# First layer of a two-layer model: a chunk's key-value sum ahead of its outputs, and the state updated by one VectorE operation per head

## The chip, the cores and the metric

The kernel runs on one core of a Trainium2 chip. The metric is the device time of one execution in microseconds; of the kernel before there are five runs, and their median counts. A profile is one more execution, recorded instruction by instruction. Engines are named as in the profile: PE (TensorE, matmuls; PEld are its weight loads), DVE (VectorE), ACT (ScalarE), POOL (GpSimd), SP (SyncE, which issues DMAs).

## The reference, cut to what matters

Two layers run one after the other on x of 2 x 2048 x 256. The change is in the attention of the first layer, a gated linear attention with two heads of 128:

```python
def step(S, inp):
    qt, kt, vt, gt = inp
    S = jnp.exp(gt)[..., None] * S + kt[..., None] * vt[..., None, :]
    ot = jnp.einsum('bhd,bhde->bhe', qt, S)
    return (S, ot)
```

The state S (128 x 128 per head) decays by a factor per row and takes in the outer product of key and value; the output is the query times the state. Beside it the first layer quantises the normed input in blocks of 32 (`_mx_quantize`) and multiplies it by a quantised weight. The output of the attention is gated, normed (`_layernorm`) and projected, and both are added to x. The second layer (softmax attention, then experts) follows and is not touched.

## The kernel before, in words

**Tiling.** The 4096 tokens are cut into 8 strips of 512 (`Strip`, 0 to 3 for the first sequence, 4 to 7 for the second), a strip into four chunks of 128. Inside a chunk the decay is folded into queries and keys, so that a chunk's output is two products per head: masked weights x values (`attn`, `v`), and query x state. The state is kept scaled so that one factor per row and head, `to_next`, carries it to the next chunk: new state = (state + keys x values) x `to_next`. The factor is a product of two columns of `spans`, which ScalarE fills in `queries()` (L675) before the strip's chunks run.

**A chunk (`chunk(n)`, L765 to L804).** One PSUM tile `both` (named o_ds_ps in the profile, two buffers) holds the outputs `o_ps` and the key-value sums `ds_ps`. TensorE does, per head, weights x values and query x state into `o_ps`, then both heads' keys x values into `ds_ps`. Each float32 product is two matmul instructions in the trace, some 0.11 us apart. VectorE makes `to_next` (L792, 128x2) and adds state and `ds_ps` for both heads into `sum` (L796, 128x256). ScalarE scales `sum` by `to_next`, one operation per head (L799, 128x128), which is the new state. VectorE then multiplies the gate by `o_ps` into `og` (L801) and takes its statistics (L119, L121). Chunk 0 of a sequence has no state before it (`none`), and the last chunk of a sequence makes none.

**What sets the order.** The strips are woven together by hand in the loop from L867. For strip s the order of pieces is: `weights()` of s; `values_gates()` of s+1 (products vf_ps); then chunk 0, chunk 1, `queries()` of s+1 (products q_ps and c_ps, on VectorE `arg` L680 and L681 and q L683, on ScalarE `ls` and the exponential of `arg` L682), chunk 2, chunk 3; between them the four steps of the quantisation of s+1 (`mx_steps`, L149), which alternate VectorE (L180 to L188, L193, L196) and GpSimd (L191, L194, L197); then the norm of `og` (`norm_o`: GpSimd L128, VectorE L130), the query and key products of the second layer for s-1 (qk_ps), the transposes of `og` (tr, L565), `keys()` of s+1, `sum_up()` (y_ps), and so on. The matmuls are kept in program order by `mm` (L514). On VectorE, ScalarE and GpSimd a scheduler puts the instructions in an order of its own when the kernel is built, except for those pinned; each engine then runs its list in order. Waits are counts of finished instructions on another engine.

**Strips that differ.** Strip 0 also quantises the weight (`quantised_weight`, tile wd, and its copies by ScalarE L596). Strip 4 starts a sequence. Strip 7 has no strip after it, so its four chunks follow each other with no quantisation and no queries between them.

Of the kernel before, what the change touches and what calls it, by code (L numbers as in the profile page):

```python
# [53 lines left out]
F32 = mybir.dt.float32  # L54
# [3 lines left out]
ALU = mybir.AluOpType  # L58
# [3 lines left out]
P = 128  # L62
# [5 lines left out]
HG = 2  # L68
# [184 lines left out]
@with_exitstack  # L253
def usual_way(ctx, tc, a, out, c, blocks):
    nc = tc.nc
    keep = ctx.enter_context(tc.tile_pool(name="keep", bufs=1))
    acc = keep.tile([P, NT, E], F32, tag="acc", name="acc")
    la = keep.tile([P, NT, NE], F32, tag="la", name="la")
    norms = keep.tile([P, 1, NSTRIP], F32, tag="norms", name="norms")
    spans = keep.tile([P, NSTRIP, HG, 4, 2], F32, tag="spans", name="spans")  # L260
    operands = Operands(nc, keep, a, c)
    ready = Constants(nc, keep, a, c)

    fill = Fill(nc, keep, a, out, c)

    def besides(s):

        if s == 0:
            fill.begin()
            operands.make_first()  # L270
            ready.load()
        elif s < NSTRIP - 2:
            fill.rows(s - 1, NSTRIP - 3)
        elif s == NSTRIP - 2:
            operands.load_first()

    with tc.tile_pool(name="proj", bufs=1) as pool:
        layer0(tc, a, acc, spans, c, operands, Projections(tc, pool, a, c, norms, la), besides)
    later = ctx.enter_context(tc.tile_pool(name="later", bufs=1))
    routing = Routing(nc, later, a, c)  # L280
    attention(tc, a, out, acc, la, norms, spans, c, operands, ready, routing, blocks)
# [217 lines left out]
def layer0(ctx, tc, a, acc, spans, c, operands, projections, besides):  # L499
# [6 lines left out]
    nc = tc.nc  # L506
# [3 lines left out]
    p2 = ctx.enter_context(tc.tile_pool(name="l0p2", bufs=2))  # L510
# [3 lines left out]
    def mm(*args, **kwargs):  # L514
        tc.keep_in_program_order(nc.tensor.matmul(*args, **kwargs))  # L515
# [82 lines left out]
    class Strip:  # L598


        def __init__(self, s):
            self.s = s
            self.ts = slice(4 * s, 4 * s + 4)
            self.x = acc[:, self.ts, :]
            self.first = s % (NSTRIP // B) == 0
            self.last = (s + 1) % (NSTRIP // B) == 0

        def norm_x(self):
            self.xn = p2.tile([P, 4, E], F32, tag="xn", name="xn", bufs=1)
            norm = LayerNorm(nc, p2, expo, "x")  # L610
            norm.see(self.x, 0)
            norm.apply(self.xn, self.x)
            nc.gpsimd.tensor_tensor(
                self.x, self.x, ffnb.unsqueeze(1).to_broadcast([P, 4, E]), ALU.add
            )
# [121 lines left out]
        def weights(self):  # L737
# [24 lines left out]
            self.og = p2.tile([P, 4, E], F32, tag="og", name="og", bufs=1)  # L762
            self.norm = LayerNorm(nc, p2, expo, "o")

        def chunk(self, n):  # L765

            nonlocal state
            s = self.s
            both = ps_s.tile([P, 2, HG, P], F32, tag="sm", name="o_ds_ps")
            o_ps, ds_ps = both[:, 0, :, :], both[:, 1, :, :]  # L770
            none = self.first and n == 0
            for h in range(HG):
                hs = slice(h * P, (h + 1) * P)
                mm(
                    o_ps[:, h, :], lhsT=self.attn[:, h * 4 + n, :], rhs=self.v[:, n, hs],
                    start=True, stop=none,
                )
                if not none:
                    mm(
                        o_ps[:, h, :], lhsT=self.q[:, h, n * P : (n + 1) * P],  # L780
                        rhs=state[:, h, :], start=False, stop=True,
                    )
            if not (self.last and n == 3):
                for h in range(HG):
                    hs = slice(h * P, (h + 1) * P)
                    mm(
                        ds_ps[:, h, :], lhsT=self.kt[:, n, hs], rhs=self.v[:, n, hs],
                        start=True, stop=True,
                    )
                after = spans[:, s, :, n + 1, 0] if n < 3 else spans[:, s + 1, :, 0, 0]  # L790
                to_next = p2.tile([P, HG], F32, tag="to_next", name="to_next")
                nc.vector.tensor_tensor(to_next, spans[:, s, :, n, 1], after, ALU.mult)  # L792
                sum_ = ds_ps
                if not none:
                    sum_ = p2.tile([P, HG, P], F32, tag="sum", name="sum")
                    nc.vector.tensor_tensor(sum_, state, ds_ps, ALU.add)  # L796
                new = p2.tile([P, HG, P], F32, tag="state", name="state", bufs=3)
                for h in range(HG):
                    nc.scalar.mul(new[:, h, :], sum_[:, h, :], to_next[:, h : h + 1])  # L799
                state = new  # L800
            nc.vector.tensor_tensor(  # L801
                self.og[:, n, :], self.gate[:, n, :], o_ps.rearrange("p h d -> p (h d)"), ALU.mult
            )
            self.norm.see(self.og[:, n : n + 1, :], n)  # L804
# [43 lines left out]
        def greatest(self):  # L848
            projections.greatest(self.s, self.squares, ps_m, mm)

    state = None
    nc.scalar.preload_act_table_set("natural_log_exp_and_others")
    strips = [Strip(s) for s in range(NSTRIP)]

# [12 lines left out]
    for s, now in enumerate(strips):  # L867
        after = strips[s + 1] if s + 1 < NSTRIP else None
# [1483 lines left out]
```

## Time and profile before

| what | us |
|---|---|
| median of 5 runs | 1775.18 (1772.32 to 1777.95) |
| the profiled execution, its time | 1772.8 |
| its span, first to last instruction | 1770.9 |
| first layer in it | up to about 450 |
| busy in the span: PE / DVE / ACT / POOL | 1671.4 / 694.3 / 804.7 / 392.3 |
| one strip (vf_ps of one to vf_ps of the next) | 50.1 |
| chunk 0 of strip 2 / of strip 7 begins | 163.2 / 406.8 |

A row of a timeline or of a chain begins with its start and its length in us from the start of the span; then come engine, line, operation, tile written <- tiles read, and shape. In square brackets stands how long the engine was idle before it and what ended that. A row of a tile or line view has min/median/max of one instruction in ns. A row of the waits has the total, the number of times and the longest, in us. A wait is put down to the event that came last before it ended, and this is only where the reader starts: that event can itself have been held up by an older one in its engine's queue, which the chain of waits follows back.

### The profile page before, as it was taken

Reading aid. Unit: us, or ns where it says so; the run is one execution under the profiler, and the core shown is the slowest. Engines: PE = TensorE matmul, PEld = TensorE weight load, DVE = VectorE, ACT = ScalarE, POOL = GpSimd, SP = SyncE. Lnnn points to the kernel's source line nnn. Section 1 sums busy time; section 2 is a strip of 40 time slices with the busy share of each in tenths; the row PEclk is TensorE's granted clock in tenths of the full one; section 3 lists DMA queues with packets and bytes.
Section 4 is the critical chain, followed back from the end, with each engine's and each line's share of the span. In section 5 each row is a group of like instructions: output and inputs, shape, how many; then the busy total and the mean of one; then the engine's idle time right before and its main releaser. Section 6 shows DMA issues by size and latency. Waiting matters only on the chain.

```text
span 1770.9 us, 31816 instructions
## 1 busy us (share of the span) xinstructions
PE 1671.4 (94%) x13314; PEld 1296.1 (73%) x13314; DVE 694.3 (39%) x1798; ACT 804.7 (45%) x1590; POOL 392.3 (22%) x350
## 2 busy tenths in 40 slices
PE   4699999998999989999999999999999999999995
PEld 2467666665666656766766688898888888889885
DVE  7877667653554663232242222222222222222221
ACT  2344554544778767978988911111111112111110
POOL 4332222211200003324300012222222222222211
PEclk9899999999999999999999999999999999999998
DMA  9501114104600401442130175556555555557521
GB/s 268 154 24 38 50 50 101 50 24 110 137 10 1 78 13 63 101 111 66 51 124 14 43 269 169 164 176 214 176 178 188 181 182 194 164 177 237 164 84 17
DMA packets 82505, 204.33 MB, mean 115 GB/s; under 512 B 8624, under 2 KB 64304, under 8 KB 71728
## 3 DMA queue, kind: packets, MB, share of 16 engines
q0 software_dynamic: 24944, 138.33, 24.1%
q1 hardware_dynamic: 56304, 62.71, 13.2%
q8 instruction: 106, 1.74, 0.4%
q10 hardware_dynamic: 1104, 1.18, 0.2%
q14 instruction: 47, 0.39, 0.1%
HBM read 152.26 MB, written 49.92 MB: 114 GB/s over the span
## 4 chain that ended last, share of the span: by engine, by line
PE 83%; DVE 9%; ACT 4%; POOL 1%; DMA 1%; issue 1%; SPq 0%; POOLq 0%; DVEq 0%
PE h_ps L2113 27%; PE y_ps L2129 13%; PE sc L1687 11%; PE o_ps L1718 10%; PE y_ps L515 3%; PE qk_ps L515 3%; ACT pt L1693 3%; PE vf_ps L515 2%; PE f_ps L1670 2%; PE vg_ps L515 2%; PE tr L565 2%; DVE pt L1705 2%; PE g_ps L515 1%; PE o_tr L1644 1%; PE o_ds_ps L515 1%; PE x_ps L2091 1%
## 5 line engine op out<-in xcount | busy, mean ns | idle before, releaser
L1693 ACT ACTIVATE pt<-sc,shift 128x512 f32<-128x512 f32 (+3 forms) x832 | 464.7, 680 | 100.0 <-PE sc L1687 98.0
L2113 PE MATMUL h_ps<-va,qk 128*128 128x256 f32 (+1 forms) x2368 | 484.3, 365 | 0.0
L2113 PEld LDWEIGHTS h_ps<-va,qk 128*128 128x128 f32 x2368 | 425.4, 190 | 53.3 <-ACT va L2095 0.2
L2118 ACT ACTIVATE sg<-h_ps 128x256 f32<-128x256 f32 (+1 forms) x296 | 109.4, 370 | 593.5 <-PE h_ps L2113 591.7
L1687 PE MATMUL sc<-qk 32*128 32x256 f32 (+6 forms) x3680 | 277.9, 370 | 4.2 <-DVE onT L1664 1.7
L2119 DVE TENSOR_TENSOR larger<-sg,h_ps 128x256 f32<-128x256 f32 (+1 forms) x296 | 119.3, 403 | 355.4 <-ACT sg L2118 332.7
L1687 PEld LDWEIGHTS sc<-qk 32*128 32x128 f32 x3680 | 202.1, 187 | 63.4 <-ACT pt L1693 27.8
L1718 PE MATMUL o_ps<-pt,va 128*32 128x256 f32 (+7 forms) x3680 | 230.0, 353 | 17.5 <-DVE o_sb L1751 17.5
L1718 PEld LDWEIGHTS o_ps<-pt,va 128*32 128x32 f32 x3680 | 122.4, 110 | 97.0 <-issue 29.9
L2138 POOL DMA_INDIRECT out<-va,to x69 | 110.1, 1596 | 216.7 <-DMA out<-va,to 69.6
L1705 DVE TENSOR_TENSOR pt<-pt,keepmask 128x1024 f32<-128x1024 f32 x64 | 78.5, 1226 | 185.6 <-ACT pt L1693 185.6
L2129 PE MATMUL y_ps<-qk,larger 128*128 128x256 f32 x560 | 124.3, 379 | 1.0 <-DVE va L2134 1.0
L2129 PE MATMUL y_ps<-larger 128*128 128x256 f32 x544 | 120.4, 379 | 0.0
L2129 PEld LDWEIGHTS y_ps<-qk,larger 128*128 128x128 f32 x560 | 104.8, 190 | 14.8 <-DVE va L2134 1.4
L2134 DVE SCALAR_TENSOR_TENSOR va<-y_ps,wt,half_bias 128x256 f32<-128x256 f32 x69 | 30.4, 480 | 209.9 <-PE y_ps L2129 209.9
L2129 PEld LDWEIGHTS y_ps<-larger 128*128 128x128 f32 x544 | 102.0, 190 | 13.1
L2023 POOL DMA_INDIRECT table<-rows,place x64 | 65.8, 1028 | 172.8 <-DMA table<-rows,place 134.8
L2053 POOL DMA_INDIRECT qk<-in_wgateup,wrow x37 | 37.3, 1007 | 298.5 <-PE h_ps L2113 152.4
L515 PE MATMUL vf_ps<-qk,xnT 128*128 128x512 f32 x128 | 58.3, 609 | 0.0
L515 PE MATMUL o_ds_ps<-state,q 128*128 128x128 f32 x120 | 25.6, 296 | 22.8 <-ACT state L799 22.8
L515 PEld LDWEIGHTS vf_ps<-qk,xnT 128*128 128x128 f32 x128 | 24.1, 194 | 29.0 <-issue 27.0
L1675 DVE TENSOR_TENSOR acc<-acc,f_ps 128x512 f32<-128x512 f32 x32 | 22.0, 687 | 56.8 <-PE f_ps L1670 56.8
(246 smaller groups left out, 1715.0 us busy)
## 6 DMA issues: line engine op xcount, KB each, us to landing
xb<-table SPq DMA_DIRECT2D x32, 265.0 KB
qk<-qk SPq DMA_DIRECT2D x32, 256.0 KB
qk<-qk SPq DMA_DIRECT2D x64, 128.0 KB
table<-spare SPq DMA_DIRECT2D x3, 2120.0 KB
va<-v SPq DMA_DIRECT2D x4, 1208.0 KB
v<-v SPq DMA_DIRECT2D x8, 574.0 KB
normed<-xn SPq DMA_DIRECT2D x8, 512.0 KB
rows<-normed POOLq DMA_DIRECT2D x16, 256.0 KB
```

The costliest lines, as they stand in the source:

```text
L515: tc.keep_in_program_order(nc.tensor.matmul(*args, **kwargs))
L1687: nc.tensor.matmul(scs[r][:, at : at + q1 - q0], lhsT=heads[rows, 1, kb * P : (kb + 1) * P], rhs=heads[rows, 0, qt * QT + q0 : qt * QT + q ...
L1693: nc.scalar.activation(pt[:, r, 0:width], scs[r][:, 0:width], AF.Exp, bias=shift)
L1705: ins = nc.vector.tensor_tensor(part, part, mask[:, 1 - way, :].unsqueeze(1).unsqueeze(1).to_broadcast([P, 4, 2, P]), ALU.min,)
L1718: nc.tensor.matmul(o_ps[r * HR : (r + 1) * HR, to + q0 : to + q1], lhsT=va[:, kb, h * VC : h * VC + HR], rhs=pt[:, r, at : at + q1 - q0], ...
L2023: self.nc.gpsimd.indirect_dma_start(out=self.c.table, in_=rows[:, n, :], in_offset=None, out_offset=bass.IndirectOffsetOnAxis(ap=to[:, 2 * ...
L2053: e.nc.gpsimd.indirect_dma_start(out=w, out_offset=None, in_=e.a[name], in_offset=bass.IndirectOffsetOnAxis(ap=e.c.wrow[:, self.b : self.b ...
L2113: nc.tensor.matmul(ps[:, j, rows], lhsT=self.wgu[:, j, c, f * P : (f + 1) * P], rhs=self.xT[:, c, rows], start=c == 0, stop=c == 1,)
L2118: nc.scalar.activation(sg, ps[:, 0, rows], AF.Silu)
L2119: nc.vector.tensor_tensor(self.hT[:, f, rows], sg, ps[:, 1, rows], ALU.mult)
L2129: nc.tensor.matmul(ps[:, c, :], lhsT=self.hT[:, fc, c * P : (c + 1) * P], rhs=self.wd[:, fc, :], start=fc == 0, stop=fc == NFC - 1,)
L2138: nc.gpsimd.indirect_dma_start(out=out, out_offset=bass.IndirectOffsetOnAxis(ap=self.to[:, c : c + 1], axis=0), in_=y[:, c, :], in_offset= ...
```

## The change

The key-value sums of a chunk are put ahead of its outputs in TensorE's order. `to_next` is made once for each chunk, by whoever asks first, and kept in a dictionary of the strip. As soon as a chunk's new state is written, ScalarE scales it by the factor of the following chunk into `kept` (`keep`, L781 in the new kernel), for the last chunk of a strip by the factor of the next strip's chunk 0. The new state of a chunk is then one VectorE operation per head, `ds_ps` x `to_next` + `kept` (L816 in the new kernel), in place of one VectorE addition for both heads and two ScalarE scalings behind it. Chunk 0 of a sequence still takes its state from ScalarE, directly from `ds_ps`. The arithmetic is the same up to rounding. The built order of VectorE, ScalarE and, in strip 0, of GpSimd changes with it; SP's does not.

```diff
+        def to_next(self, n):
+            if n not in self.factors:
+                after = spans[:, self.s + (n + 1) // 4, :, (n + 1) % 4, 0]
+                t = p2.tile([P, HG], F32, tag="to_next", name="to_next", bufs=3)
+                nc.vector.tensor_tensor(t, spans[:, self.s, :, n, 1], after, ALU.mult)
+                self.factors[n] = t
+            return self.factors[n]
+
+        def keep(self, n):
+            nonlocal kept
+            if not (self.last and n == 3):
+                kept = p2.tile([P, HG, P], F32, tag="sum", name="kept")
+                for h in range(HG):
+                    nc.scalar.mul(kept[:, h, :], state[:, h, :], self.to_next(n)[:, h : h + 1])
+
         def chunk(self, n):
...
-            for h in range(HG):
-                hs = slice(h * P, (h + 1) * P)
-                mm(
-                    o_ps[:, h, :], lhsT=self.attn[:, h * 4 + n, :], rhs=self.v[:, n, hs],
-                    start=True, stop=none,
-                )
-                if not none:
-                    mm(
-                        o_ps[:, h, :], lhsT=self.q[:, h, n * P : (n + 1) * P],
-                        rhs=state[:, h, :], start=False, stop=True,
-                    )
-            if not (self.last and n == 3):
+            final = self.last and n == 3
+
+            if not final:
                 for h in range(HG):
                     hs = slice(h * P, (h + 1) * P)
                     mm(
                         ds_ps[:, h, :], lhsT=self.kt[:, n, hs], rhs=self.v[:, n, hs],
                         start=True, stop=True,
                     )
-                after = spans[:, s, :, n + 1, 0] if n < 3 else spans[:, s + 1, :, 0, 0]
-                to_next = p2.tile([P, HG], F32, tag="to_next", name="to_next")
-                nc.vector.tensor_tensor(to_next, spans[:, s, :, n, 1], after, ALU.mult)
-                sum_ = ds_ps
+            for h in range(HG):
+                hs = slice(h * P, (h + 1) * P)
+                mm(
+                    o_ps[:, h, :], lhsT=self.attn[:, h * 4 + n, :], rhs=self.v[:, n, hs],
+                    start=True, stop=none,
+                )
                 if not none:
-                    sum_ = p2.tile([P, HG, P], F32, tag="sum", name="sum")
-                    nc.vector.tensor_tensor(sum_, state, ds_ps, ALU.add)
+                    mm(
+                        o_ps[:, h, :], lhsT=self.q[:, h, n * P : (n + 1) * P],
+                        rhs=state[:, h, :], start=False, stop=True,
+                    )
+            if not final:
                 new = p2.tile([P, HG, P], F32, tag="state", name="state", bufs=3)
+                to_next = self.to_next(n)
                 for h in range(HG):
-                    nc.scalar.mul(new[:, h, :], sum_[:, h, :], to_next[:, h : h + 1])
+                    if none:
+                        nc.scalar.mul(new[:, h, :], ds_ps[:, h, :], to_next[:, h : h + 1])
+                    else:
+                        nc.vector.scalar_tensor_tensor(
+                            new[:, h, :], ds_ps[:, h, :], to_next[:, h : h + 1], kept[:, h, :],
+                            ALU.mult, ALU.add,
+                        )
                 state = new
+                if n < 3:
+                    self.keep(n + 1)
+                else:
+                    strips[self.s + 1].keep(0)
```

## The prediction, made before the changed kernel ran

> **What bounds the kernel now.** I read the page first (TensorE is busy in nine tenths or more of nearly every slice; the first layer is the stretch up to 450 us), then the waits of TensorE from 50 to 480 us, then the chain and the timeline of single strips. A strip is 50.1 us long and repeats; the one from 154 us is my example (strip 2). The waits (total us, times, longest us):
>
> ```profile
> PE o_ds_ps L515 <- ACT state L799: 22.8, 17, 4.0
> PE tr L565 <- DVE og L130: 7.6, 4, 5.9
> ```
>
> TensorE waits 22.8 us for the state that ScalarE writes, all of it in the products query x state. By window that is 5.2 us in strip 0, 2.2 to 3.2 in strips 1 to 6, 2.2 in strip 7 (404 us). So what the change can touch is about 23 us, 1.3% of the time. Whether it may be had is told by the chain of strip 2 (start, us, what):
>
> ```profile
> 165.43 0.59 ACT state L799 x2
> ...
> 166.04 0.16 DVE to_next L792
> ...
> 166.29 0.59 DVE mx_r L193
> ...
> 166.95 1.28 POOL mx_r L194
> ...
> 170.18 1.47 POOL mx_v L197
> ...
> 172.53 1.19 DVE arg L680 x2
> ...
> 173.93 1.15 ACT arg L682 x2
> 175.07 0.30 ACT state L799
> ...
> 175.42 1.38 PE o_ds_ps L515 x10
> ```
>
> The chain does not go along TensorE between 163 and 175 us. It goes over the quantisation of the next strip, which VectorE and GpSimd hand to each other (mx_r, mx_v), because VectorE runs in order and `arg` stands behind it. The state's wait at 175.42 ends with ScalarE, but ScalarE was held by `arg`, and `arg` by that quantisation. The two waits of the strip, the VectorE work between, and what TensorE meets after them:
>
> ```profile
> 164.74 0.42 DVE L796 TENSOR_TENSOR sum<-state,o_ds_ps 128x256 f32<-128x256 f32 x1 [0.91 <-PE o_ds_ps L515]
> 165.77 0.49 PE L515 MATMUL o_ds_ps<-state,q 128*128 128x128 f32 x2 [0.84 <-ACT state L799]
> 174.59 1.28 DVE L683 TENSOR_TENSOR q<-arg,q_ps 128x512 f32<-128x512 f32 x2 [0.24 <-ACT arg L682]
> 175.42 0.49 PE L515 MATMUL o_ds_ps<-state,q 128*128 128x128 f32 x2 [1.49 <-ACT state L799]
> 183.10 0.14 PEld L565 LDWEIGHTS tr<-ident,og 128*128 128x128 f32 x1 [0.26 <-DVE og L130]
> 184.07 0.53 PEld L565 LDWEIGHTS tr<-ident,og 128*128 128x128 f32 x5 [0.18 <-DVE og L130]
> ```
>
> The last two lines matter most. The fourth transpose waits for the fourth normalised `og`, which ends at 184.01. So the second half of VectorE's chain (mx_r at 177.27, GpSimd, the norm of `og`) already ends with TensorE or 0.2 to 0.3 us after it. If TensorE comes earlier, it waits at the transposes. If that chain comes later, the strip gets longer by as much.
>
> **The change part by part.** Counts: 28 sums on VectorE (0.42 us each) become 56 operations on half the columns, one per head; ScalarE keeps its 60 scalings (0.386 us, 0.30 apart), 56 of them now of the old state; the 30 small `to_next` stay, some moved; the matmuls stay, in a new order. SP's queue and all DMAs keep their order. GpSimd's order differs in one place, in strip 0.
>
> The new operation (accumulator x scalar + SBUF operand, 128x128) has no row. The nearest has its form at twice the width:
>
> ```profile
> L2134 DVE SCALAR_TENSOR_TENSOR va<-y_ps,wt,half_bias x69: 474/483/485, 1057.2 to 1753.8; 128x256 f32<-128x256 f32 x69
> 1099.53 0.88 DVE L2134 SCALAR_TENSOR_TENSOR va<-y_ps,wt,half_bias 128x256 f32<-128x256 f32 x2 [6.14 <-PE y_ps L2129]
> ```
>
> One takes 0.483 and two start 0.40 apart. TENSOR_TENSOR rows (0.689 at 512 columns, 0.416 at 256) give 0.137 us for 128 columns, so I take 0.35 long and 0.27 apart. Bounds: 0.16 (a 128x4 row, L681) and 0.483.
> [...]
>
> What the wait counts. Accumulator and key-value sum lie in one tile (`both`). In the built program the new operation waits for a TensorE count which only the last of the chunk's six products raises. So "the sum comes first" does not release it earlier. It does let TensorE do the next chunk's two sums (0.45 us) during the wait.
>
> Strip 2, first wait. Chunk 0's products start at 163.20 and end as before; VectorE goes at 164.74. Head 0's state is there at 165.09, head 1's at 165.36, without ScalarE. TensorE has the next sums and one weight product to do until 165.2, so its wait goes from 0.84 to about 0.05, and `q_ps` starts near 165.9 instead of 166.99: 1.1 us won. VectorE then: og 165.28, statistics 165.73. The next in its queue is chunk 1's head 0, which waits for chunk 1's last product (166.13) and for the kept part (ScalarE's softplus ends at 165.42; the kept part at 165.72). Behind it stand the aggregate and mx_r, which before ran at 166.21 and now at 166.13 + 0.27 + 0.09 = 166.49. The quantisation is 0.28 late, and with it all up to `arg`.
>
> Second wait. VectorE's built order is now: arg, arg, small ones, state of head 0, q, q, state of head 1. Head 0's comes at 174.4 and does not wait for ScalarE's `arg`. But q of head 0 does: 174.59 + 0.28 = 174.87, both q take 1.20, so head 1's state starts at 176.07 and ends at 176.42; TensorE takes it at 176.48 and starts `qk_ps` at 176.81 instead of 176.64. The 1.1 us won are gone: TensorE waits twice, near 1.8 and 1.2 us, instead of once.
> Then on VectorE: og 176.34; chunk 3's head 0 waits for chunk 3's last product, 177.02; statistics 177.29; head 1 177.63; aggregate 177.90; mx_r 177.99 instead of 177.27. That is +0.72 for mx_r, the norm and the transposes, and nothing hides it: **+0.72 us** for strip 2, and for 5 and 6, whose order is the same.
>
> Others. Strip 1: ScalarE's softplus comes later (the state was at 115.24), so the first half is 0.06 early instead of 0.28 late: +0.72 - 0.34 = +0.38. Strip 3 has no new state in chunk 3; its `qk_ps` and fourth og move by +0.63. Strip 4 starts from no state; the built order has both heads ahead of q, TensorE comes 1.5 us earlier at `qk_ps` but mx_r stays (277.20 to 277.21): 0.
> Strip 7 has no next strip, so no quantisation. Three waits of this kind,
>
> ```profile
> 412.36 0.49 PE L515 MATMUL o_ds_ps<-state,q 128*128 128x128 f32 x2 [0.72 <-ACT state L799]
> ```
>
> cost 1.0 us of issue each; 0.67 us of products now cover the one VectorE operation. Chunk 3 ends near 412.6 instead of 415.4, og's norm has 3 us of slack there (ends 419.5, used 422.4): -2.85.
> Strip 0 has another VectorE order: the weight's quantisation moves behind chunk 3, and GpSimd does L613 (2.39 us) ahead of the weight's last step, which moves from 85.2 to about 88. `og` stays within 0.3; ScalarE's copy of the weight reaches `y_ps` near 89.9 instead of 89.22: +0.7, between -1 and +2.
>
> Sum: 0.7 + 0.38 + 3 x 0.72 + 0.63 + 0 - 2.85 = **+1.0 us**. With the operation at 0.16 it is about -2.2, at 0.483 about +3.2: five strips have its length once and its spacing three times on their path, so 0.06 more is some 0.2 in each and 1.0 in all. The profiled execution took 1772.8 us (span 1770.9), 2.4 below the median of 1775.18; so 1773.8 against it, and 1776.2 against the median.
>
> **Rivals.**
> *The clock falls (slower).* Place: chunk 3 of strips 1, 2, 3, 5, 6, where TensorE has two waits, 3 us in all with 0.45 us of work between. Clock rows (stretch; length, busy PE, PEld, DVE, ACT, POOL; clock; DMA):
>
> ```profile
> 70.00:72.00 2.00, 1.38 (x6) 1.38 (x7) 2.00 (x7) 0.86 (x3) 0.00 (x0) 0.50 0.00 0
> 623.00:624.00 1.00, 0.00 (x0) 0.00 (x0) 1.00 (x1) 1.00 (x3) 0.00 (x0) 0.50 0.00 0
> 274.00:276.00 2.00, 0.65 (x5) 0.65 (x6) 1.77 (x4) 1.59 (x4) 0.00 (x0) 1.00 0.01 4
> ```
>
> It fell after 4.04 us of idling (66.6 to 70.6), and at 622.9 after only 1.13 us of idling among narrow products; 2.3 us in strip 4 did not do it. After a fall some 3.7 us of work pass at half speed (83.26 to 86.9; 625.7 to 629.5): 1.85 lost, 0.55 of it slack, so 1.3 a strip, 6.5 in all five: 1782.7. It decides from one fall in two or more strips.
> [...]
> *VectorE's costs at their upper bound:* 0.48 us and more, or the head operations held by GpSimd as `to_next` is at 178.18 (1.12 us): some 0.5 us a strip on top, 1779.5. For it: two thirds of each strip's chain is VectorE. Against: `arg` reads PSUM and SBUF like the new one and was not held while L191 ran.
> *The chain has slack that I don't see (faster):* the strips gain what TensorE wins, 0.3 to 1.1 us in six strips, with 2.85 in strip 7: 1769. For it: TensorE's own start at the transposes (183.08) is level with the chain.
> *It does what it says:* all 22.8 us but the first strip's go: 1757. Against: the chain of 163 to 175 us.
>
> **Numbers.** Forecast (within 3.5 us, the 0.2% that a measurement of this kernel can tell) 0.56; clock 0.15; VectorE's upper bound 0.12; slack 0.13; does what it says 0.04. So faster 0.17, same 0.56, slower 0.27. The range takes in the bounds of the operation (-2.2 to +3.2), the clock rival and most of the slack rival: 1769.5 to 1782.
>
> **What would show it.** Right: waits for the state near 0 at chunk 1 and 3 us in two pieces at chunk 3 in strips 1, 2, 3, 5, 6, the second ended by VectorE after the second q; strip period 50.1 to near 50.8; no waits in strip 7; L816 near 0.35 us. Wrong: a period below 50 us, a granted clock of 0.5 outside strip 0 and the attention, L816 waiting behind GpSimd, or a head-1 state that comes before q.

## The result, and the profile after

The changed kernel takes 1778.5 us (median of 33 runs, 1776.27 to 1780.77); the kernel before, run beside it, 1774.55 (60 runs). The ratio is 1.002, 95% interval 1.0015 to 1.0025: slower by some 4 us. The profiled execution took 1778.7 us, span 1776.9, which is 6.0 more than the span before; that one lay 1.75 under its median.

The first row to read is TensorE's, on the page of the kernel before and of the changed kernel:

```profile
PE 1671.4 (94%) x13314; PEld 1296.1 (73%) x13314; DVE 694.3 (39%) x1798; ACT 804.7 (45%) x1590; POOL 392.3 (22%) x350
PE 1681.1 (95%) x13314; PEld 1300.7 (73%) x13314; DVE 698.0 (39%) x1826; ACT 804.1 (45%) x1590; POOL 396.0 (22%) x350
```

The number of matmuls is the same, but they are busy 9.7 us longer. TensorE is idle 3.7 us less (95.8 of 1776.9; before 99.5 of 1770.9). So the change did take idle time away, and the loss is in products that run slower. The waits of TensorE from 50 to 480 us (total us, times, longest) say the same:

```profile
PE o_ds_ps L515 <- DVE state L816: 16.8, 13, 2.0
PE tr L565 <- DVE og L130: 10.5, 5, 8.0
PE wtr L594 <- POOL wd L197: 1.4, 1, 1.4
```

The wait for the state fell from 22.8 to 16.8 (and 0.7 for ScalarE in a sequence's first chunk). Strip 2 begins 3.51 us later than before in this execution (159.74 instead of 156.23). Its timeline after:

```profile
168.25 0.61 DVE L816 SCALAR_TENSOR_TENSOR state<-o_ds_ps,to_next,kept 128x128 f32<-128x128 f32 x2 [0.91 <-PE o_ds_ps L515]
...
170.06 0.66 DVE L193 SCALAR_TENSOR_TENSOR mx_r<-mx_r,mx_pw 128x512 f32<-128x512 f32 x1
...
177.94 0.34 DVE L816 SCALAR_TENSOR_TENSOR state<-o_ds_ps,to_next,kept 128x128 f32<-128x128 f32 x1
...
178.33 0.49 PE L515 MATMUL o_ds_ps<-state,q 128*128 128x128 f32 x2 [1.50 <-DVE state L816]
178.43 1.28 DVE L684 TENSOR_TENSOR q<-arg,q_ps 128x512 f32<-128x512 f32 x2 [0.15 <-ACT arg L683]
179.63 0.35 DVE L816 SCALAR_TENSOR_TENSOR state<-o_ds_ps,to_next,kept 128x128 f32<-128x128 f32 x1
...
180.03 0.80 PE L515 MATMUL o_ds_ps<-state,q 128*128 128x128 f32 x2 [0.99 <-DVE state L816]
...
180.62 6.35 PE L515 MATMUL qk_ps<-xn2T,cwq 128*128 128x512 f32 x8
...
181.87 0.66 DVE L193 SCALAR_TENSOR_TENSOR mx_r<-mx_r,mx_pw 128x512 f32<-128x512 f32 x1
...
187.23 1.39 DVE L130 TENSOR_SCALAR og<-og,ln_mvo,ln_rstdo 128x256 f32<-128x256 f32 x4 [0.80 <-POOL ln_rstdo L128]
...
190.24 1.04 PE L565 MATMUL tr<-ident,og 128*128 128x128 f32 x8
```

The wait at chunk 1 is gone. At chunk 3 there are two, 1.50 and 0.99 us, the second behind both q. Then the eight qk_ps products take 6.35 us; before they took 3.60:

```profile
176.64 3.60 PE L515 MATMUL qk_ps<-xn2T,cwq 128*128 128x512 f32 x8
```

The transposes no longer wait for `og` (ready at 188.62): TensorE comes to them only at 190.24. The same stretch by windows of 3.41 us (length, busy PE, PEld, DVE, ACT, POOL; granted clock, that is the share of its full speed that TensorE was allowed; DMA), the kernel before in the first two rows, then the changed one:

```profile
172.30:175.71 3.41, 1.93 (x17) 1.74 (x16) 3.18 (x10) 1.91 (x5) 1.27 (x1) 1.00 0.00 0
175.71:179.12 3.41, 3.41 (x16) 2.07 (x16) 3.25 (x9) 1.26 (x3) 1.11 (x1) 1.00 0.00 0
...
172.53:175.94 3.41, 3.41 (x30) 3.17 (x29) 2.43 (x7) 1.55 (x5) 1.46 (x1) 1.00 0.00 0
175.94:179.35 3.41, 1.60 (x12) 1.22 (x11) 3.26 (x11) 1.44 (x3) 1.26 (x1) 1.00 0.00 0
179.35:182.76 3.41, 2.73 (x5) 1.60 (x6) 2.85 (x10) 1.21 (x3) 0.15 (x1) 0.50 0.00 0
182.76:186.18 3.42, 3.42 (x5) 1.35 (x4) 2.31 (x6) 1.32 (x2) 2.13 (x3) 0.50 0.10 40
186.18:189.59 3.41, 3.41 (x9) 1.52 (x8) 1.56 (x5) 2.15 (x4) 1.01 (x2) 1.00 0.29 114
```

The clock is 0.50 for exactly two windows. It falls in strips 1, 2, 3, 5 and 6 of the changed kernel (at 128.1, 179.3, 233.9, 336.3 and 387.5), not in strip 4, and nowhere in strips 1 to 6 before. Two more falls of 3.41 us, at 42.8 ahead of strip 0 and at 90.6 in strip 0, are in this profile alone. By strip (vf_ps to vf_ps, us):

| strip | before | after | difference | predicted | half clock, us |
|---|---|---|---|---|---|
| 0 | 57.13 | 58.30 | +1.17 | +0.7 | 17.07, and 3.41 more (17.07 before) |
| 1 | 51.00 | 51.95 | +0.95 | +0.38 | 3.41 |
| 2 | 50.11 | 53.04 | +2.93 | +0.72 | 6.83 |
| 3 | 49.37 | 51.72 | +2.35 | +0.63 | 3.41 |
| 4 | 50.56 | 50.56 | 0.00 | 0 | none |
| 5 | 50.11 | 51.72 | +1.61 | +0.72 | 3.41 |
| 6 and 7, to the first sc | 94.10 | 92.95 | -1.15 | +0.72 - 2.85 | 3.41 (strip 6) |

The sum is +7.86, and strip 0 began 1.39 later (0.45 later at 42.25, ahead of the fall at 42.8, and 1.39 behind it). The rest of the program then ran 3.25 faster than in the profile before: some 1.5 across a fall of the clock at 455.6, of 3.41 us, which the profile before has and this one has not, and 1.3 behind TensorE's last product; the remaining 0.5 I leave open. That makes the 6.0.

The clock is lower in the other executions too: over the whole execution its mean is 0.977 to 0.980 in every one of the changed kernel (median 0.979), and 0.979 to 0.985 (median 0.982) in 25 of the kernel before, run beside the first four experiments. As an estimate from these two medians, 0.003 of 1777 us is some 5 us, the size of the loss.

### The profile page after: what moved, and what is told of

The parts are those of the page before. It is cut to its first block, busy times and chain, and to the rows that moved or that the text cites. A ratio compares the mean times of both kernels' runs of the same rounds, so it can differ in the third digit from the quotient of the medians.

```text
span 1776.9 us, 31863 instructions
## 1 busy us (share of the span) xinstructions
PE 1681.1 (95%) x13314; PEld 1300.7 (73%) x13314; DVE 698.0 (39%) x1826; ACT 804.1 (45%) x1590; POOL 396.0 (22%) x350
## 3 DMA queue, kind: packets, MB, share of 16 engines
q8 instruction: 107, 1.75, 0.4%
## 4 chain that ended last, share of the span: by engine, by line
PE 83%; DVE 9%; ACT 4%; POOL 1%; DMA 1%; issue 1%; SPq 0%; POOLq 0%; DVEq 0%
PE h_ps L2137 27%; PE y_ps L2153 13%; PE sc L1711 11%; PE o_ps L1742 10%; PE qk_ps L515 4%; PE y_ps L515 3%; ACT pt L1717 3%; PE vf_ps L515 2%; PE f_ps L1694 2%; DVE pt L1729 2%; PE vg_ps L515 2%; PE g_ps L515 2%; PE tr L565 2%; PE o_tr L1668 1%; PE o_ds_ps L515 1%; PE x_ps L2115 1%
## 5 line engine op out<-in xcount | busy, mean ns | idle before, releaser
L515 PE MATMUL o_ds_ps<-state,q 128*128 128x128 f32 x120 | 26.5, 304 | 17.7 <-DVE state L816 16.8
```

## The experiments

**Theory A:** most of the loss is TensorE's clock, which falls at chunk 3 because the state's wait there is in two pieces. **Rivals:** B, the order of the products costs, whoever makes the state; C, only the second head's place behind q costs (0.72 us a strip) and the clock is a by-product; D, the operation from the accumulator is dear wherever it stands. The last column compares with the runs of the kernel before beside each group; "middle" is from the start of strip 1 to the first sc of the attention, in the profiled execution (345.25 before, 351.94 after), and leaves out loading, strip 0 and the attention.

| run | median us | middle us | falls in strips 1 to 6 | ratio (95%) |
|---|---|---|---|---|
| e1 order alone | 1769.3 | 343.81 | strip 4 | 0.9968 (0.9956 to 0.998) |
| e2 state alone | 1779.47 | 351.20 | 2, 4, 6 | 1.003 (1.0017 to 1.0042) |
| e3 both waits filled | 1772.65 | 344.44 | none | 0.999 (0.9981 to 0.9999) |
| e4 q later | 1770.78 | 342.65 | 3 | 0.9976 (0.9965 to 0.9986) |
| e5 order, new state in strip 7 | 1765.35 | 338.89 | none | 0.9951 (0.9936 to 0.9967) |
| e6 order, g1 moved | 1752.75 | 329.71 | none | 0.9877 (0.986 to 0.9893) |
| e7 as e5, g1 moved | 1755.6 | 329.76 | 1 | 0.9889 (0.9874 to 0.9903) |
| e8 changed kernel, g1 moved | 1760.09 | 332.05 | none | 0.9917 (0.9901 to 0.9932) |
| e9 second wait filled | 1776.48 | 348.16 | 1, 3, 6 | 1.0004 (0.9994 to 1.0013) |
| e10 q later, g1 moved | 1759.56 | 331.23 | none | 0.9907 (0.9892 to 0.9922) |
| e11 before, g1 moved | 1762.65 | 334.37 | none | 0.9927 (0.9914 to 0.9941) |
| e12 e6, new state in strip 7 | 1754.99 | 331.19 | 1 | 0.9894 (0.9879 to 0.9909) |

"Middle" holds strip 7 as well, and there, ahead of the attention, e1, e2, e3, e4, e10, e11 and e12 have one more fall of 3.41 us, which neither the kernel before nor the changed one has. Strip 0's half clock differs too (17.07 us in the profile before, 20.48 in the one after), so medians and "middle" carry falls that no edit aimed at; what an edit does is read from single strips.

### The change's two parts: e1 and e2

e1 is the kernel before with the two sums moved:

```diff
+                for h in range(HG):
+                    mm(ds_ps[:, h, :], lhsT=self.kt[:, n, hs], rhs=self.v[:, n, hs], ...)
                 for h in range(HG):
                     mm(o_ps[:, h, :], lhsT=self.attn[...], ...)
                     mm(o_ps[:, h, :], lhsT=self.q[...], rhs=state[:, h, :], ...)
-                for h in range(HG):
-                    mm(ds_ps[:, h, :], lhsT=self.kt[:, n, hs], rhs=self.v[:, n, hs], ...)
```

> The kernel before with one part of the change: the two key-value sums stand ahead of the chunk's four output products; the state is still one sum on VectorE and two scalings on ScalarE. Theory A (most of the loss is TensorE's clock falling in chunk 3, and it falls because the state's wait there is in two pieces, one per head): here ScalarE writes both heads' states 0.3 us apart, so the wait stays in one piece; 0.45 us of sums go into each of some 14 waits, while VectorE's chain ends a strip as before. Waits for the state 15 to 20 us instead of 22.8, no stretch with granted clock 0.5 in strips 1 to 6, time 1772 to 1775.5 (-0.1% to 0 against the kernel before). Rival B (the order of the products is what costs, whoever makes the state): at least +3 us, 1777.5 or more, and falls as in the changed kernel.

It went further than that: 1769.3. Rival B is out. One point was missed: the clock did fall in strip 4, where a single wait of 2.58 us put 2.05 us of idling into one window. Strip 2's wait is as long as before and in one piece, but the sums are already done when the state comes, so qk_ps starts 19.95 us into the strip instead of 20.41:

```profile
172.12 0.49 PE L515 MATMUL o_ds_ps<-state,q 128*128 128x128 f32 x2 [1.48 <-ACT state L800]
...
172.89 3.60 PE L515 MATMUL qk_ps<-xn2T,cwq 128*128 128x512 f32 x8
```

The strip is 0.55 shorter; strips 1 and 5 likewise (0.52 and 0.55). Half of the whole gain is strip 0's (-2.68); how much of that is its quantised weight and how much its clock was not taken apart.

e2 is the changed kernel with the sums put back behind the outputs.

> The changed kernel with the old order of the products: outputs first, the two sums behind them; the state is one VectorE operation per head on the part kept by ScalarE. Theory A: the second head's state still stands behind both q products on VectorE, so chunk 3's wait is still in two pieces, and with the sums no longer in them they are longer by some 0.2 to 0.45 us: the clock falls to 0.5 in strips 1, 2, 3, 5 and 6 or most of these, time 1778 to 1782 (+3.5 to +7 us against the kernel before). Rival C (the extra wait alone, the clock is only a sign of it): +1 to +2 us, 1775.5 to 1776.5. Rival B (order of the products): within 1 us of the kernel before.

1779.47, as theory A has it, but the clock fell in strips 2, 4 and 6 only: in two of the five that were named, although 1, 3 and 5 have the same two waits as 2 (1.16 and 1.06 us), and in strip 4, which wasn't named (1.95 and 0.99). Windows of 3.41 us laid on the grid of the falls show what differs (strip 2, then strip 3):

```profile
172.99:176.40 3.41, 1.40 (x11) 1.02 (x9) 3.18 (x10) 1.44 (x3) 1.27 (x1) 1.00 0.00 0
176.40:179.81 3.41, 3.20 (x9) 2.17 (x10) 2.39 (x9) 0.93 (x3) 0.35 (x1) 0.50 0.00 0
224.19:227.60 3.41, 1.95 (x16) 1.57 (x14) 3.18 (x11) 1.15 (x2) 1.27 (x1) 1.00 0.00 0
227.60:231.01 3.41, 2.65 (x8) 1.46 (x9) 3.19 (x11) 0.41 (x1) 0.30 (x1) 1.00 0.00 0
```

In strip 2 both waits lie in one window: busy 1.40, idle 2.01, and the next window has half the clock. In strip 3 the window's edge cuts them: 1.46 idle on one side, 0.76 on the other, and the clock stays at 1.00. What tells the two strips apart is the idle time within a window, not the number of pieces.

### The clock: e3 and e9

Both add products to the changed kernel which are overwritten by the real ones, at chunk 3 of strips 1, 2, 3, 5 and 6:

```diff
+WARM = (5, 3)  # e3; e9: (0, 3)
             for h in range(HG):
+                for _ in range(WARM[h] if n == 3 and self.s in (1, 2, 3, 5, 6) else 0):
+                    mm(o_ps[:, h, :], lhsT=self.kt[:, n, hs], rhs=self.v[:, n, hs], start=True, stop=True)
                 mm(o_ps[:, h, :], lhsT=self.attn[...], ...)
```

> The changed kernel with added products whose results are overwritten (128x128 each, 5 ahead of head 0's output product and 3 ahead of head 1's, in chunk 3 of strips 1, 2, 3, 5, 6 only): TensorE works during the two waits, the state comes when it did. One thing moves beside it: the built order now puts the second mx_r ahead of both of chunk 3's state operations in most strips, which is worth 0.3 us a strip. Theory A: no stretch with granted clock 0.5 in strips 1 to 6, and the time falls by what the falls cost, 3 to 6 us below the changed kernel: 1772.5 to 1775.5. Rival C (the falls cost nothing, because the products behind them have slack or VectorE's chain is the bound anyway): 1777 to 1779, as the changed kernel, or a little above from the added 8 x 0.23 us where they outlast the waits.

More work on TensorE, and 5.85 us less time: 1772.65, inside theory A's range; rival C is out. Not all of it is the clock, since the built order moved too. Strip 2 takes 53.04 us in the changed kernel, 50.89 in e9 below, which keeps the changed kernel's order on VectorE and has no fall there, and 50.22 here: by that comparison 2.15 are the fall and 0.67 the order. Over strip 2 the clock stays whole:

```profile
176.00:180.00 4.00, 3.29 (x17) 2.28 (x17) 3.81 (x13) 1.76 (x5) 0.28 (x1) 1.00 0.01 4
180.00:184.00 4.00, 4.00 (x10) 1.71 (x9) 2.36 (x8) 3.36 (x7) 2.71 (x3) 1.00 0.26 101
```

e9 fills the second wait alone.

> As the run with overwritten products, but with only the 3 ahead of head 1's output product in chunk 3 of strips 1, 2, 3, 5, 6 (0.7 us of work in the second wait of 1.0 us); the first wait of 1.5 us stays. VectorE's built order there is the changed kernel's (both state operations of chunk 3 ahead of the second mx_r). Theory A as the split wait: a single wait of 1.5 us does not drop the clock (the kernel before has one of 1.49 us in each strip), so no granted clock of 0.5 in strips 1 to 6 and 1772 to 1775.5. Rival I (the first wait, or the order on VectorE, is enough, and the second wait is beside the point): falls as in the changed kernel and 1777 to 1779.5.

A half miss: 1776.48, over theory A's range. Strips 2 and 5, with a first wait of 1.5 us, kept the clock as expected; strips 1 and 3, whose first wait is 1.90 and 1.95, lost it to that alone, and strip 6 to 1.29 and 0.40 in one window (1.68 idle). Strip 2, then strip 3, on this run's grid:

```profile
174.29:177.70 3.41, 1.90 (x17) 1.71 (x17) 2.88 (x11) 0.79 (x2) 1.61 (x2) 1.00 0.00 0
177.70:181.11 3.41, 3.09 (x16) 2.05 (x16) 3.16 (x10) 1.83 (x5) 0.00 (x0) 1.00 0.00 0
225.49:228.90 3.41, 1.47 (x13) 1.27 (x12) 3.19 (x11) 1.11 (x2) 1.29 (x2) 1.00 0.00 0
228.90:232.31 3.41, 3.41 (x12) 2.42 (x11) 2.92 (x10) 0.04 (x1) 0.00 (x0) 0.50 0.00 0
```

So theory A's "in two pieces" falls and is replaced: here the clock fell after windows with 1.68 (in two pieces), 1.90 and 1.94 us of idling (one piece each), and not after those with 1.51 and 1.49 in strips 2 and 5. e9 gives something else as well: strips 2 and 5 have VectorE's order of the changed kernel and no fall. They take 50.89 and 50.88 us, +0.78 and +0.77 against before; the prediction worked out +0.72 for that order. Strip 2:

```profile
177.47 0.49 PE L515 MATMUL o_ds_ps<-state,q 128*128 128x128 f32 x2 [1.51 <-DVE state L823]
...
179.17 0.49 PE L515 MATMUL o_ds_ps<-state,q 128*128 128x128 f32 x2 [0.32 <-DVE state L823]
...
180.71 0.66 DVE L193 SCALAR_TENSOR_TENSOR mx_r<-mx_r,mx_pw 128x512 f32<-128x512 f32 x1
...
186.53 0.14 PEld L565 LDWEIGHTS tr<-ident,og 128*128 128x128 f32 x1 [0.83 <-DVE og L130]
```

mx_r is 21.83 us into the strip (21.04 before), and the transposes wait 0.83 for `og`: the late chain is what the strip pays.

### The order on VectorE: e4

```diff
                 nc.scalar.activation(arg, arg, AF.Exp)
-                nc.vector.tensor_tensor(self.q[:, h, :], arg..., ps, ALU.mult)
+                self.pending.append((h, arg, ps))   # queries_end() does them
...
         now.chunk(2)
+        if after:
+            after.queries_end()
```

> The changed kernel with the two q products of the next strip written behind chunk 2 in the program, so that on VectorE both heads' state operations of chunk 2 stand together ahead of q, and og of chunk 2 too. Theory A: chunk 3's wait is one again, some 1.5 to 2.0 us, the clock doesn't fall in strips 1 to 6, and mx_r comes some 0.5 us earlier than in the changed kernel: 1769 to 1773, below the kernel before by 1.5 to 5 us (strip 7's 2.85 us remain won). Rival C (the clock is no cause; the place of the second head's state costs 0.72 us a strip at most): 1774.5 to 1776. Rival D (VectorE's operation from the accumulator is what is dear wherever it stands): 1777 to 1779.

1770.78, within theory A's range; rival D is out for the kernel as it was changed. Strip 2:

```profile
174.95 0.60 DVE L821 SCALAR_TENSOR_TENSOR state<-o_ds_ps,to_next,kept 128x128 f32<-128x128 f32 x2
175.34 0.49 PE L515 MATMUL o_ds_ps<-state,q 128*128 128x128 f32 x2 [1.50 <-DVE state L821]
...
175.79 0.67 DVE L689 TENSOR_TENSOR q<-arg,q_ps 128x512 f32<-128x512 f32 x1
...
176.11 3.60 PE L515 MATMUL qk_ps<-xn2T,cwq 128*128 128x512 f32 x8
...
183.30 1.73 PE L565 MATMUL tr<-ident,og 128*128 128x128 f32 x8 [0.16 <-DVE og L130]
```

Both heads' states come together, qk_ps starts 19.35 us into the strip, 1.06 earlier than before, and only 0.33 of it is left in the strip (49.78 for 50.11), because the transposes now wait for `og` (eight of them take 1.73 us; in the changed kernel, where they don't wait, 1.04). In strip 3 a single wait of 1.94 dropped the clock here too.

### Real work in the wait: e5 to e8, e10 to e12

If idle time at chunk 3 is what hurts, real products belong there. Those into g1 need only the next strip's xnT:

```diff
         now.chunk(2)
+        if after:
+            after.gates()
...
             after.quantised_columns()
-            after.gates()
```

e11 does this to the kernel before, e6 to e1, e8 to the changed kernel, e10 to e4. e5 is e1 with the new form of the state in strip 7 alone; e7 is e5, and e12 is e6, with both.

> The new order of the products with the old form of the state, and one move of real work: the next strip's four products into g1 (1.7 to 1.9 us, they need only xnT of the next strip) stand between chunk 2 and chunk 3, where TensorE waits some 1.3 to 2.6 us for ScalarE's state, instead of late in the strip. Theory F (a strip is as long as TensorE's work and waits, VectorE's chain has some slack in that build: og ended 0.5 us before the kernel before's in strip 2): 1.2 to 1.5 us less in each of six strips, 1760 to 1763. Rival G (the prediction's: VectorE's chain to the fourth og is level with TensorE, so what is filled here is waited for at the transposes): 1767 to 1770, with waits of the transposes for og of 1 us or more a strip.

> The changed kernel with the g1 products (1.7 to 1.9 us) between chunk 2 and chunk 3 instead of late in the strip. The state's two waits there, 1.5 and 1.0 us, become one of about 1.0 or less. Theory A: no stretch with granted clock 0.5 in strips 1 to 6, so it falls at least as far as the run with the overwritten products (1772.7): 1764 to 1773, the lower part if a strip is as long as TensorE's work, the upper if VectorE's chain holds it. Rival C (the clock is not what costs): 1776 or more.

> The kernel before, untouched but for the g1 products between chunk 2 and chunk 3. It parts what that move brings by itself from what the new order of the products adds. If a strip is as long as TensorE's work and waits: 1.5 us less in each of six strips, 1762 to 1766, 9 to 13 us above the run of the new order with g1 moved (1752.75), because the other waits, 0.84 us at chunk 1 and those of strips 0 and 7, stay. If the order of the products adds nothing once the wait of chunk 3 is filled: 1752 to 1756.

All three came out as low as expected or lower: 1752.75 (theory F 1760 to 1763), 1760.09 (1764 to 1773), 1762.65 (1762 to 1766). Strip 2 of e6:

```profile
168.53 1.88 PE L515 MATMUL g_ps<-xnT,qk 128*128 128x512 f32 x4
...
170.41 0.68 ACT L800 ACTIVATE state<-sum,to_next 128x128 f32<-128x128 f32 x2
...
170.91 0.42 PE L515 MATMUL o_ds_ps<-state,q 128*128 128x128 f32 x2
...
171.62 3.60 PE L515 MATMUL qk_ps<-xn2T,cwq 128*128 128x512 f32 x8
...
178.49 1.04 PE L565 MATMUL tr<-ident,og 128*128 128x128 f32 x8
```

The product with the state has no bracket: no wait. qk_ps starts 19.96 us into the strip, as in e1 (19.95), so the work stands exactly where the wait was; the strip is shorter by its length behind the transposes (47.58 for 49.56). I had put the gain at the wait (1.2 to 1.5 a strip); it is the moved work and 0.2 at the transposes, 1.98. Rival G forgot that work moved from behind the transposes to ahead of them is won even where the transposes are set by `og`. Against e11 the order of the products is worth another 0.45 in strip 2 and 2.5 in strip 0.

> The kernel with the new order of the products everywhere and the old form of the state (one sum on VectorE, two scalings on ScalarE), except in the last strip, which alone has the new form. In the run of the new order alone, strip 7 still waits 0.28, 0.28 and 0.72 us for ScalarE's state; with the new form one wait of 0.25 is left in the changed kernel. Theory A (in strip 7 nothing of the next strip stands in VectorE's queue, so the new form pays there): 1.0 us less than the new order alone (1769.3), 1767.3 to 1769. Rival E (strip 7's end is set by the norm of og, not by TensorE): 1769 to 1770.5.

> Both together: the new order, the new form of the state in strip 7 alone, and the g1 products between chunk 2 and chunk 3. The two edits lie in different strips, so their gains should add: theories A and F 1759 to 1762; A with rival G 1766 to 1769.

> The new order of the products with the old form of the state, g1 moved, and the new form in strip 7 alone, written so that the built order of strips 0 to 6 is that of the run with the new order and g1 moved. Expected that run's time less strip 7's waits of 0.28, 0.28 and 0.72 us and a fall of the clock behind them: 1750 to 1752, strip 0 at 54.4 us. Rival E: 1752.5 to 1754.

> The changed kernel with both cures: the two q products written behind chunk 2, so that no q stands between the heads' states on VectorE, and the g1 products between chunk 2 and chunk 3. If the new form of the state costs nothing by itself once it stands well (theory A), strips 1 to 6 are as long as in the run of the new order with g1 moved (47.6 us) and strip 7 is shorter: 1751 to 1756, with strip 0 some 2 to 4 us longer than there. Rival D (the operation from the accumulator is dear wherever it stands): strips of 48.4 us, as in the changed kernel with g1 moved, 1757 to 1761.

e5 came out lower than expected (1765.35): from the start of strip 6 to the end of the last chunk it takes 55.89 us, 1.47 less than e1 (57.36; before 59.32), and the clock didn't fall in strip 4 this time. e7 and e12 do not beat e6: in both the clock fell in strip 1, in e12 in strip 7 too, and e7's strip 0 is 4.3 longer than e6's. e12 lies above both of its ranges. The intervals of e6 and e12 overlap; e6 is the simplest of the best. e10 is a miss for theory A: 1759.56 lies in D's range, and its strip of 48.00 between the two. Strip 2's qk_ps starts 0.6 earlier than in e6, but `og` is normed from 26.08 us into the strip instead of 25.50, and the transposes wait. Two of the new operations hold VectorE 0.60 us where one sum takes 0.41; whether that or the new place of q makes the chain late was not separated.

An accumulator tile of its own for the sums, with which VectorE might start before the chunk's last product, wasn't tried; what it would bring is not shown.

## Why the prediction was right or wrong

The time lies in the range, only 2.3 us above the forecast's 1776.2, and that is in part luck: against the kernel before that ran beside it the change costs 4.0 us where the forecast had 1.0, and what makes up the difference is the clock, which the forecast left out. In the profiled pair the forecast's terms for strips 0 to 7 add up to 1.0 and the strips lost 7.86. Point by point:

- **The new operation** was put at 0.35 us long and 0.27 apart. It has 0.345, and two take 0.61. Right. The row:

```profile
L816 DVE SCALAR_TENSOR_TENSOR state<-o_ds_ps,to_next,kept x56: 319/345/353, 61.3 to 424.1; 128x128 f32<-128x128 f32 x56
```

- **The first wait**: gone, and mx_r at 166.49 predicted, 166.55 measured (170.06 less 3.51). Right.
- **The second wait in two pieces**: head 1's state at 176.07 predicted, 176.12 measured. The waits are 1.50 and 0.99 instead of "near 1.8 and 1.2". Right in mechanism, 0.5 long in size.
- **"That is +0.72 ... and nothing hides it"**: right, but only e9 shows it (+0.78 and +0.77). In the changed kernel itself mx_r comes 22.13 us into the strip, 1.09 late: 0.79 as in e9, and 0.30 more with chunk 3's last products ahead of it at half clock. TensorE at half clock came to the transposes 1.6 us after `og`, so this term is hidden by a larger one. Strip 2's +2.93 is: qk_ps starts 0.47 later, the way from there to the transposes is 9.62 instead of 6.87 us, and 0.29 of waiting for `og` is gone.
- **Strip 4 at 0 and strip 7 at -2.85**: 0.00; and in e4, where strip 7 can be read without a fall ahead of it, strips 6 and 7 to the end of the last chunk take 3.19 less, 0.40 of it up to strip 7's first a_ps product. That leaves -2.79. Right in size; 0.36 of it is chunk 0's wait for `attn`, which the sums now cover and the prediction did not count.
- **Strip 0**: +1.17 for +0.7, and that is luck. The prediction had the weight's copy reach `y_ps` 0.7 later. Measured from the strip's start it came 0.87 earlier (40.25 us into the strip for 41.12). Then the clock fell at 90.6, and from the first y_ps product to k_tr TensorE took 9.06 us for 7.01.
- **The clock: this is the step that failed.** The rival was described in full: its place (strips 1, 2, 3, 5, 6), its price (1.3 a strip, 6.5 in all), its point of decision (two falls or more). It came in all five, and they cost 6.4 us together in the profiled execution (each strip's excess over the predicted term: 0.57, 2.21, 1.72, 0.89, 0.98). Only its chance was wrong, 0.15, and so it stood at nothing in the sum; a granted clock of 0.5 outside strip 0 and the attention was also the prediction's own sign of being wrong. It was weighed by the longest single idle stretch: 4.04 us dropped the clock (at 69.90, in fact, with 0.7 us of the stretch still to come), 2.3 us in strip 4 did not. In the runs the falls of strips 1 to 7 went with the idle time in windows of 3.41 us: after all 14 windows with 1.94 us or more, after none of 25 with 1.33 to 1.64. The 2.3 us of strip 4 lie across an edge:

```profile
271.28:274.69 3.41, 1.77 (x16) 1.58 (x15) 3.18 (x11) 1.01 (x3) 1.26 (x1) 1.00 0.00 0
274.69:278.11 3.42, 2.76 (x14) 1.98 (x15) 3.25 (x10) 1.60 (x5) 0.17 (x1) 1.00 0.01 2
```

1.64 idle and 0.65: no evidence that 2.3 is safe. The row at 622.9, which did fall without a long stretch, was the warning.
- **Why 1778.5 and not the rival's 1782.7**: in the profiled pair the strips lost 7.86 us: the forecast's 1.0, 6.4 for the five falls, and 0.5 in strip 0. At the end 6.0 were left, after a fall at the start of the attention that only the profile before has, and that profile was itself 1.75 under its median. In e2 the place of a window's edge decided between a fall (strip 2) and none (strip 3), so by estimate other executions have other sums; their mean clock goes from 0.977 to 0.980.

## What to carry to other kernels

Sum TensorE's idle time over some 3.4 us (the falls here begin on steps of 3.413) before calling a wait short: splitting the wait did not help here, where 1.7 to 2.5 us of idling stayed in one such window, and it cost 0.6 to 2.2 us each time. Compare TensorE's busy time at an equal count of matmuls between two profiles: a rise, as here (9.7 us at 13314 matmuls), sends one to the granted clock, even when the waits have become shorter. And look for work that could stand in the wait before making the wait's cause faster: moving 1.7 us of products into it gave 12 us to the old kernel and 18 to the changed one.

## What the runs showed of the hardware that I had not expected

- Every fall in strips 1 to 6 lasted 3.41 us or twice that (6.83), and within a run the falls begin on a grid: in the changed kernel at 128.13, 179.33, 233.94, 336.34 and 387.54, which are 15, 16, 30 and 15 steps of 3.413 apart. In the profiles of both kernels all falls between 30 and 700 us (6 before, 12 after) lie on one such grid for each profile, to within 0.01 us; in e1, e2, e3, e4 and e9 so do those between 95 and 470 us (e1: 271.24, 431.66 and 448.73, 47 and 5 steps apart).
- How much idling a window takes: of the windows on these grids that begin between 95 and 430 us in the fourteen profiles (both kernels and the twelve runs), none of 25 with 1.33 to 1.64 us of idle TensorE was followed by a fall, 5 of 9 with 1.68 to 1.90 were, and all 14 with 1.94 to 2.65. So in these rows about half of a window was enough, and no window that led to a fall was wholly idle. "About half" is drawn from these rows alone. What decides in the mixed band stays open.
- Idle time is not the whole measure. Where the attention begins, with products of 32 rows (sc), the clock fell after windows with 1.2 to 1.4 us of idling (e1, e2, e3, e4, e9), and in the profile before at 455.6 after one with 0.40. Further on in the changed kernel's attention it fell at 585.5 after 1.33, and did not after windows with 1.86 (from 558.21) and 1.57 (from 616.24). No run was made to find out why.
- The clock comes back at an edge as well. Strip 2's fall lasted two windows: in the first of them TensorE was still idle for 0.68 us, the second was all busy (the rows of 179.35 and 182.76 above). In strips 1 to 6, where the first window of a fall was busy for 2.89 us (e1, strip 4) or more, it was the only one. At the attention it was otherwise: in e1, e2, e3, e4 and e9 the fall lasted two windows (6.83 us) although TensorE was idle for at most 0.08 us of the first.
